# Three 512x512 products of a four-layer graph kernel as seven block products each, with streamed weights

## The chip, the cores and the metric

One core of a Trainium2 chip runs the whole kernel in one launch. The metric is the device time of that launch in microseconds. The kernel before took 2557.84 us (median of three runs, 2553.96 to 2559.38).

A core has five engines that run side by side, each through its own list of instructions in order: TensorE (PE; matrix products, with PEld for loading its stationary operand), VectorE (DVE), ScalarE (ACT), GpSimd (POOL) and SyncE (SP, which here only issues transfers). They wait for each other on semaphores. Matrix products land in PSUM, eight banks of 128 x 512 float32, which VectorE and ScalarE read.

## The reference

Four graph layers over 128 graphs of 64 nodes with 512 features, float32 throughout; after each layer the input is added and the sum normalised over the features:

```
x = layernorm(x + L0(x));  x = layernorm(x + L1(x));  ...  L3

L0: s = (x @ w) @ a
    A = exp(leaky(8 tanh((s_i + s_j)/8))) * adj          leaky(t) = t if t >= 0 else 0.1 t
    A = A / rowsum(A) * rowsum(adj);   out = A @ x @ w
L1: weight = adj * exp((x Wq^T + bq)(x Wk^T + bk)^T), rows divided by their sums
    out = weight @ (x Wv^T + bv)
L2: w_i = <q_i, (adj @ k)_i> / sqrt(512);   out = softmax(w) * (x @ Wv)
L3: two hypergraph convolutions with H = (adj != 0):
    conv(x, W, b) = Dn * (H @ (Be * (H^T @ (x @ W^T)))) + b
    h = layernorm(relu(conv(x, W1, b1)));   out = conv(h, W2, b2) + x
```

W1 is 1024 x 512 and W2 is 512 x 1024; the other weights are 512 x 512 (Wqk holds two).

## The kernel before

**Tiles and groups.** The 8192 node rows make 64 tiles of 128 rows (two graphs each); a group is two tiles (`GT = 2`), so there are 32 groups. A chunk is eight tiles, four groups; `prepare_chunk` works out what depends on `adj` alone for a chunk: `bhd` (H divided by both degrees), `am`, `radj` (the row sums of adj), `g1`.

**One group** is the generator `run(g)`, cut by `yield` into stages. Layer 0: scores and `exp`, placed on a block diagonal (`on_diagonal`, L474); the aggregation of x with it, transposed (`gathered`, L362), and the row sums by four matmuls with a column of ones (`row_sums`, L403), whose reciprocal times `radj` is the factor `f`; then the product with w0 (`product`, L370: per tile four accumulating matmuls of 128x128 by 128x512) and one VectorE instruction per tile that scales by `f` and adds x (L506); then `layer_norm` (statistics L459, L460, L450; the power on POOL, L452; L463). Layer 1: transposed x (`transposed`, L352), the row dot with `u1_b` on VectorE (L469), the bias added on POOL (L519); `product_T` with the prepared matrix m1 (L379, 16 matmuls of 256 columns); v by `product` with wv1, copied by ScalarE (L524); scores (L394), `exp`, and the aggregation (L537, L538). Layer 2: transposed x, `product_T` with m2, scores, a softmax over each graph (L565 to L579) that gives the factor `wc`, and v by `product` with wv2, scaled and added in one VectorE instruction per tile (L582). Layer 3: an aggregation, a product 512 to 1024 ("3a"), relu and normalisation, an aggregation (L626), a product 1024 to 512 ("3b"), the last `layer_norm`, the store.

**Seven products.** 3a and 3b already run in a form that uses seven block products in place of eight. Left and right side are cut into 2 x 2 blocks (left: two tiles by two halves of the contraction; right: two halves of the rows by two of the columns). `side_sums` (L408 to L411) forms four sums of left blocks, three on VectorE and one on POOL. The right sides, three plain blocks and four sums `t1` to `t4`, are made once at the start. `seven_products` multiplies pair by pair into PSUM: bank x (`chx`) collects three products in turn, z (`chz`) two, and the two y products go to the general banks `mm`. VectorE reads x after its first, second and third product, and z after each of its two; TensorE may add to a bank only after the read before.

**Streamed weights.** The seven right sides of 3a and 3b are 512 KB each. `fetch` loads them one after the other from DRAM, in the order of use, into a ring of six tiles on SP's queue; each product releases its tile and calls for the next fetch. w0, wv1 and wv2 stay in the core's memory for the whole run and are loaded at the start by POOL's queue. SP's queue also carries the loads of x and adj and the stores of the result.

**Order.** Four groups are in flight, four steps apart; in each step every group in flight goes on by one stage, in an order of ages that the loop writes out (youngest first, but in every fourth step the two oldest first). A scheduler in the language layer then sets the order on each engine, so matmuls of one stage stand between those of another; an engine goes through the resulting list strictly in order. PSUM: three banks `mm`, one `chx`, one `chz`, two `tr` (transposes and aggregations), one `sm` (small results).

Of the kernel before, what the change touches and what calls it, by code (L numbers as in the profile page):

```python
# [10 lines left out]
FP = mybir.dt.float32  # L11
# [4 lines left out]
P = 128  # L16
# [9 lines left out]
RING = 6  # L26
PIECE = 1024
EPS = 1e-5
# [5 lines left out]
def kernel(  # L34
# [99 lines left out]

    load_adj(0)
    load(0)
    w0_sb = weights(w0, D, D, "w0_sb")
# [10 lines left out]
    wv1_sb = weights(wv1, D, D, "wv1_sb")  # L148
    bv1_b = bcast(bv1, D, "bv1_b")
    wqk_g = wqk2.rearrange("(h c p) o -> h p c o", h=2, p=P)  # L150
    wv2_sb = weights(wv2, D, D, "wv2_sb")
# [22 lines left out]
    def prepare_0():  # L174

        u = small.tile([P, KC], FP, name="u0")
        for c in range(KC):
            row_dot(u[:, c : c + 1], w0_sb[:, c, :], 1.0, a0_b)
        ps = ps_mm.tile([P, D], FP, name="mm")
        for c in range(KC):  # L180
            nc.tensor.matmul(ps[:, ts(c, P)], u[:, c : c + 1].to_broadcast([P, P]), ident, start=True, stop=True)
        nc.scalar.copy(u0_b, ps)
# [35 lines left out]
    USE = ("b11", "b21", "t1", "t2", "b22", "t4", "t3")  # L218
    pieces = {}

    def piece_tile():
        return ring.tile([P, PIECE], FP, name="piece")

    def quarters(w, rows, cols):

        v = w.rearrange("(h c p) (i o) -> h i p c o", h=2, p=P, i=2)
        return {f"b{h + 1}{i + 1}": v[h, i] for h in range(2) for i in range(2)}

    def load_quarters(w, rows, cols):
        made = {}  # L230
        for name, src in quarters(w, rows, cols).items():
            made[name] = piece_tile()
            nc.sync.dma_start(out=made[name].rearrange("p (c o) -> p c o", o=cols // 2), in_=src)
        return made

    def combined(q):
        t1, t2 = piece_tile(), piece_tile()
        nc.gpsimd.tensor_sub(t1, q["b12"], q["b11"])
        nc.vector.tensor_sub(t2, q["b22"], t1)
        t3 = piece_tile()  # L240
        nc.gpsimd.tensor_sub(t3, q["b22"], q["b12"])
        t4 = piece_tile()
        nc.vector.tensor_sub(t4, q["b21"], t2)
        return {"t1": t1, "t2": t2, "t3": t3, "t4": t4}

    def stored(name, tiles):
        made = {}
        for k, t_ in tiles.items():
            made[k] = dram.tile([P, PIECE], FP, name=f"{name}_{k}")
            nc.sync.dma_start(out=made[k], in_=t_)  # L250
        return made

    def prepare_3a():
        q = load_quarters(w3a, D, DH)
        pieces["a"] = {**quarters(w3a, D, DH), **stored("w3a", combined(q))}

    def prepare_3b():
        q = load_quarters(w3b, DH, D)
        half = KH // 2

        ps = ps_mm.tile([P, D], FP, name="mm")
        for i in range(2):
            for c in range(KH):
                b = q[f"b{c // half + 1}{i + 1}"]
                nc.tensor.matmul(ps[:, ts(i, D // 2)], beta_c[:, c : c + 1].to_broadcast([P, P]),
                                 b[:, ts(c % half, D // 2)], start=(c == 0), stop=(c == KH - 1))
        nc.scalar.copy(bw_b, ps)
        for i in range(2):
            for c in range(KH):
                b = q[f"b{c // half + 1}{i + 1}"][:, ts(c % half, D // 2)]  # L270
                nc.vector.tensor_scalar(b, b, gamma_c[:, c : c + 1], None, ALU.mult)
        kept = stored("w3b", {k: q[k] for k in ("b11", "b21", "b22")})
        pieces["b"] = {**kept, **stored("w3b", combined(q))}
# [3 lines left out]
    fetched = [0]  # L277

    def fetch():
        n = fetched[0]  # L280
        fetched[0] += 1
        if n >= NG * 2 * len(USE):
            return
        which = "ab"[n // len(USE) % 2]
        src = pieces[which][USE[n % len(USE)]]
        t_ = piece_tile()
        dst = t_
        if len(src.shape) == 3:
            dst = t_.rearrange("p (c o) -> p c o", c=src.shape[1])
        nc.sync.dma_start(out=dst, in_=src)  # L290
        on_chip.append(t_)
# [14 lines left out]
    def prepare_chunk(c):  # L306
# [25 lines left out]
        bhd = chunks.tile([P, CT, N], FP, name="bhd")  # L332
        nc.gpsimd.tensor_mul(bhd, hA, per_tile(be))
        nc.gpsimd.tensor_mul(bhd, bhd, dn)
# [5 lines left out]

        am = chunks.tile([P, CT, N], FP, name="am")
        nc.gpsimd.tensor_mul(am, adj, per_tile(m))
        nc.vector.tensor_mul(am, am, over_graph(md))
        prepared[c] = adj, bhd, am, radj, g1
# [53 lines left out]
    def row_sums(e):  # L398

        ps = ps_sm.tile([P, GT, P], FP, name="sm")  # L400
        for t in range(GT):
            for h, (rows, _) in enumerate(halves):
                nc.tensor.matmul(ps[rows, t, 0:1], e(t, h), ones[rows], start=True, stop=True)  # L403
# [9 lines left out]
    def seven_products(a, s, base, dst):  # L413

        n = a["11"].shape[1]

        def times(ps, left, first, last):
            b = on_chip.popleft().rearrange("p (c o) -> p c o", c=n)
            for k in range(n):
                nc.tensor.matmul(ps, left[:, k, :], b[:, k, :], start=first and k == 0, stop=k == n - 1,  # L420
                                 skip_group_check=True)
            fetch()


        w = PIECE // n
        x = ps_ch.tile([P, D], FP, name="chx")[:, :w]
        y = ps_mm.tile([P, D], FP, name="mm")[:, :w]
        z = ps_ch.tile([P, D], FP, name="chz")[:, :w]
        add = nc.vector.tensor_add
        times(x, a["11"], True, False)  # L430
        add(dst["11"], x, base["11"])  # L431
        times(y, a["12"], True, True)
        add(dst["11"], y, dst["11"])
        times(z, s[0], True, False)
        add(dst["22"], z, base["22"])  # L435
        times(x, s[1], False, False)
        add(dst["12"], x, base["12"])
        times(z, s[3], False, True)
        add(dst["12"], z, dst["12"])  # L439
        y = ps_mm.tile([P, D], FP, name="mm")[:, :w]  # L440
        times(y, a["22"], True, True)
        add(dst["21"], y, base["21"])
        times(x, s[2], False, True)
        add(dst["22"], x, dst["22"])
        add(dst["21"], x, dst["21"])
# [25 lines left out]
    def on_diagonal(dst, e, adj):  # L471

        for rows, cols in halves:
            nc.vector.tensor_mul(dst[rows, :, cols], e[rows], adj[rows])  # L474
# [3 lines left out]
    def run(g):  # L478
        xt = xs.pop(g)
        adj, bhd, am, radj, g1 = prepared[g // GC]  # L480
        own = ts(g % GC, GT)
        adj, bhd, am, radj, g1 = adj[:, own], bhd[:, own], am[:, own], radj[:, own], g1[:, own]
# [15 lines left out]
        bd = on_diagonal(next_e(), e, adj)  # L498
        yield
        gT = gathered(xt, bd)  # L500
        f = small.tile([P, GT], FP, name="f")
        nc.vector.reciprocal(f, row_sums(lambda t, h: bd[halves[h][0], t, halves[h][1]]))
        nc.vector.tensor_mul(f, f, radj)
        yield
        for t in range(GT):
            nc.vector.scalar_tensor_tensor(xt[:, t, :], product(gT, t, w0_sb), f[:, t : t + 1], xt[:, t, :],  # L506
                                           ALU.mult, ALU.add)
# [202 lines left out]
```

## Time and profile before

| | |
|---|---|
| median of three runs | 2557.84 us |
| profiled execution | 2556.45 us |
| its span, first to last instruction | 2554.7 us |
| granted TensorE clock, mean | 0.995 |
| TensorE / weight loads busy | 2487.9 / 1644.5 us |
| VectorE / ScalarE / GpSimd busy | 1361.2 / 586.2 / 620.9 us |
| products with w0 (L370, 512 records) | 226.6 us |
| products with wv1 and wv2 (L370, 1024 records) | 450.6 us |
| HBM read / written | 266.65 / 22.54 MB |
| a 512 KB fetch, issue to landing | 4.1 to 4.3 us |

A line of the groups gives line, engine, operation, output<-input, shapes and count; then the busy time of the group in us and the mean length of one in ns; then the engine's idle time just before them and who ended it. Each float32 matmul of the program stands as two records of TensorE, so 768 matmuls of 512 columns are 1536 records. Matmuls are pipelined and a single length overlaps the next, so the price of a series is read from starts: the start of the next series less the start of this one.

A line of the timeline gives start and length in us, engine, line, operation, operands, how many instructions were merged, and in brackets the idle time ahead with its releaser.

### The profile page before, as it was taken

What the parts mean: (1) busy time and instruction counts of PE and PEld (TensorE: products, weight loads), DVE (VectorE), ACT (ScalarE), POOL (GpSimd) and SP (SyncE); (2) the same over time, 40 slices, a digit from 0 to 9 for tenths busy, and PEclk for the clock granted to TensorE, in tenths of its full rate; (3) what the DMA queues carried; (4) which work ended last, traced back from release to release, by engine and by line L of the source; (5) the groups of instructions that cost most, each with busy time, mean ns of one, the idle gap of its engine ahead of it and who ended that gap; (6) DMA issues with size and microseconds to landing.
All of it is one profiled execution on the core that took longest, in us unless ns stands there. A gap on an engine that the chain in (4) does not pass through costs nothing.

```text
span 2554.7 us, 31593 instructions
## 1 busy us (share of the span) xinstructions
PE 2487.9 (97%) x12440; PEld 1644.5 (64%) x12440; DVE 1361.2 (53%) x3012; ACT 586.2 (23%) x1164; POOL 620.9 (24%) x623
## 2 busy tenths in 40 slices
PE   6999999999999999999999999999999999999997
PEld 4466667666667666667666666666667666666665
DVE  3355455565545575445655545565544566544564
ACT  0122222222222222222222222222222222222221
POOL 4122222122222132222322223122212222212321
PEclk9999999999999999999999999999999999999999
DMA  7122332343232342233333242343233343233254
GB/s 256 33 108 85 110 128 85 126 132 100 95 132 86 120 145 83 99 132 102 117 124 100 91 136 91 115 132 110 84 129 100 107 132 116 86 120 117 77 179 140
DMA packets 102740, 291.24 MB, mean 114 GB/s; under 512 B 8944, under 2 KB 10992, under 8 KB 102592
## 3 DMA queue, kind: packets, MB, share of 16 engines
q1 hardware_dynamic: 100144, 280.53, 32.9%
q0 software_dynamic: 2448, 8.70, 1.0%
q8 instruction: 98, 1.61, 0.3%
q14 instruction: 50, 0.41, 0.0%
HBM read 266.65 MB, written 22.54 MB: 113 GB/s over the span
## 4 chain that ended last, share of the span: by engine, by line
PE 76%; DVE 10%; POOL 4%; issue 2%; DMA 2%; ACT 0%; POOLq 0%; DVEq 0%; ACTq 0%
PE mm L370 21%; PE mm L379 17%; PE chx L420 10%; PE chz L420 7%; PE mm L420 7%; PE tr L362 4%; PE tr L626 3%; PE sm L394 3%; DVE x L463 2%; POOL rstd L452 2%; DMA piece<-w3b_t 2%; PE tr L352 2%; PE mm L537 1%; POOL junk L593 1%; DVE ve L450 1%
## 5 line engine op out<-in xcount | busy, mean ns | idle before, releaser
L379 PE MATMUL mm<-xT,m_sb 128*128 128x256 f32 x2048 | 457.2, 381 | 3.8 <-DVE dn L325 3.4
L370 PE MATMUL mm<-wv_sb,xT 128*128 128x512 f32 x1024 | 450.6, 592 | 0.0
L379 PEld LDWEIGHTS mm<-xT,m_sb 128*128 128x128 f32 x2048 | 387.6, 190 | 73.8 <-issue 20.1
L370 PEld LDWEIGHTS mm<-wv_sb,xT 128*128 128x128 f32 x1024 | 191.8, 190 | 214.0 <-issue 212.1
L452 POOL TENSOR_TENSOR rstd<-ve,mhalf 128x2 f32<-128x2 f32 x160 | 124.5, 778 | 782.8 <-DVE ve L450 766.8
L420 PE MATMUL chz<-piece,h 128*128 128x256 f32 (+1 forms) x768 | 246.0, 455 | 15.0 <-DVE x L435 14.1
L542 DVE TENSOR_SCALAR hT<-adj 128x128 f32<-128x128 f32 x32 | 7.2, 228 | 468.0 <-PE sm L553 468.0
L370 PE MATMUL mm<-w_sb,xT 128*128 128x512 f32 x512 | 226.6, 594 | 0.0
L420 PEld LDWEIGHTS chz<-piece,h 128*128 128x128 f32 x768 | 143.0, 190 | 97.5 <-issue 51.7
L353 ACT COPY xT<-tr 128x512 f32<-128x512 f32 x128 | 68.9, 589 | 575.4 <-PE tr L352 575.4
L420 PE MATMUL chx<-piece,h 128*128 128x256 f32 (+1 forms) x640 | 181.3, 422 | 3.0 <-DVE x L431 2.1
L463 DVE TENSOR_SCALAR x<-x,mv,rstd 128x512 f32<-128x512 f32 x256 | 141.7, 595 | 76.1 <-POOL rstd L452 76.1
L459 DVE BATCH_NORM_STATS2 st<-x 128x6 f32<-128x512 f32 x256 | 176.1, 688 | 3.4
L370 PEld LDWEIGHTS mm<-w_sb,xT 128*128 128x128 f32 x512 | 97.3, 191 | 121.1 <-issue 120.9
L594 POOL TENSOR_SCALAR x<-x 128x512 f32<-128x512 f32 x64 | 44.1, 689 | 531.3 <-PE tr L362 531.3
L610 ACT ACTIVATE h<-h 128x512 f32<-128x512 f32 x128 | 80.6, 630 | 334.2 <-DVE h L439 151.9
L420 PEld LDWEIGHTS chx<-piece,h 128*128 128x128 f32 x640 | 121.4, 190 | 47.5 <-issue 30.1
L519 POOL TENSOR_TENSOR x<-x,bv_b 128x512 f32<-128x512 f32 x64 | 81.4, 1293 | 226.8 <-PE tr L352 223.9
L626 PE MATMUL tr<-g_bd,h 128*128 128x128 f32 x1024 | 123.3, 279 | 5.8 <-ACT h L617 5.8
L420 PE MATMUL mm<-piece,xT 128*128 128x512 f32 x256 | 128.7, 606 | 0.0
L626 PEld LDWEIGHTS tr<-g_bd,h 128*128 128x128 f32 x1024 | 120.4, 194 | 8.5 <-ACT h L617 8.1
L420 PE MATMUL mm<-piece,ghT 128*128 128x256 f32 x512 | 121.0, 379 | 0.0
(174 smaller groups left out, 3271.0 us busy)
## 6 DMA issues: line engine op xcount, KB each, us to landing
piece<-w3a_t SPq DMA_DIRECT2D x128, 512.0 KB, 4.3
piece<-w3b_t SPq DMA_DIRECT2D x128, 512.0 KB, 4.3
piece<-in_w3a_dram SPq DMA_DIRECT2D x100, 512.0 KB, 4.3
piece<-w3b_b SPq DMA_DIRECT2D x96, 512.0 KB, 4.1
x<-in_x_dram SPq DMA_DIRECT2D x32, 512.0 KB, 3.4
out_dram<-x SPq DMA_DIRECT2D x32, 512.0 KB, 2.8
adj<-in_adjT_dram SPq DMA_DIRECT2D x8, 256.0 KB, 3.6
wv_sb<-in_wv_dram POOLq DMA_DIRECT2D x2, 1024.0 KB, 18.7
```

The costliest lines, as they stand in the source:

```text
L353: nc.scalar.copy(xT[:, :, ts(t, P)], tr)
L362: nc.tensor.matmul(tr[:, c, :], xt[:, t, ts(c, P)], bd[:, t, :], start=True, stop=True)
L370: nc.tensor.matmul(ps, lhsT[:, k, ts(t, P)], w[:, k, cols], start=(k == 0), stop=(k == chunks - 1))
L379: nc.tensor.matmul(pz[:, : GT * P], w[:, k, ts(c, P)], xT[:, k, :], start=(k == 0), stop=(k == KC - 1))
L394: nc.tensor.matmul(ps[rows, t, :N], zT[:, k, tok], xT[:, k, tok], start=(k == 0), stop=(k == KC - 1))
L420: nc.tensor.matmul(ps, left[:, k, :], b[:, k, :], start=first and k == 0, stop=k == n - 1, skip_group_check=True)
L452: nc.gpsimd.tensor_tensor(rstd, ve, mhalf, ALU.pow)
L459: nc.vector.bn_stats(st[:, t, :], xt[:, t, :])
L463: nc.vector.tensor_scalar(xt[:, t, :], xt[:, t, :], mv[:, t, 0:1], rstd[:, t : t + 1], ALU.subtract, ALU.mult)
L519: nc.gpsimd.tensor_add(xt[:, t, :], xt[:, t, :], bv1_b)
L610: nc.scalar.activation(hi, hi, AF.Relu)
L626: nc.tensor.matmul(tr[:, c, :], h[:, t, ts(i * KC + c, P)], gm[:, t, :], start=True, stop=True)
```

## The change

Three further products take the seven-product form: w0 of layer 0, v of layer 1 and v of layer 2.

- `seven_products` gets functions for what is done with a finished block: `first` when a bank is read for a block's first part, `more` when something is added to it. For w0, v2 and layer 3 both are a VectorE instruction that scales the bank by a per-row factor and adds (`scaled_add`); for v of layer 1 `first` is a ScalarE copy and `more` a VectorE add. Bank z is filled second instead of third.
- `left_side` forms the side sums of these products in a tile `sums`, a stage ahead of the product.
- The right sides of w0 and both v are seven blocks of 256 KB, kept in DRAM two to a tile (four fetches a product); each group fetches them again. The ring has eight tiles. The fetch order over all groups is worked out ahead (`turns`, `to_come`).
- w0 and wv1 are loaded in halves into ring tiles and combined there (`prepare_first`); v2, 3a and 3b are loaded into the large tiles `h` by SP's queue, stored, combined in place and stored again (`prepare_later`). The combination has one subtraction on POOL and three on VectorE, where it had two and two.
- Layer 0: exp(A) * adj is summed over each graph by one matmul with the block matrix `same`, its reciprocal is taken over 128 x 128 and multiplied in before the aggregation, so the factor after the product is `radj` alone. That takes one stage more; the youngest group runs two stages in its first step.
- `bhd` becomes `bh` (one degree only); the other degree `dc` is a column and is multiplied in by `scaled_add` after the products of layer 3.

```diff
-RING = 6
+RING = 8
@@ seven_products
-        times(x, a["11"], True, False)
-        add(dst["11"], x, base["11"])
-        times(y, a["12"], True, True)
-        add(dst["11"], y, dst["11"])
-        times(z, s[0], True, False)
-        add(dst["22"], z, base["22"])
-        times(x, s[1], False, False)
-        add(dst["12"], x, base["12"])
-        ...
+        first("11", times(x, a["11"]))
+        first("22", times(z, s[0]))
+        more("11", times(ps_mm.tile([P, D], FP, name="mm"), a["12"]))
+        first("12", times(x, s[1], False))
+        more("12", times(z, s[3], False))
+        first("21", times(ps_mm.tile([P, D], FP, name="mm"), a["22"]))
+        u = times(x, s[2], False)
+        more("22", u)
+        more("21", u)
+    def left_side(xT):
+        a = left_blocks(xT)
+        room = work.tile([P, 4, KC // 2, P], FP, name="sums")
+        s = [room[:, i] for i in range(4)]
+        side_sums(s, a)
+        return a, s
+    def scaled_add(dst, ps, f, k, base):
+        t = int(k[0]) - 1
+        nc.vector.scalar_tensor_tensor(dst, ps, f[:, t : t + 1], base, ALU.mult, ALU.add)
@@ run, layer 0
-        bd = on_diagonal(next_e(), e, adj)
+        nc.vector.tensor_mul(e, e, adj)
+        yield
+        nc.tensor.matmul(ps, same, e.rearrange("p t i -> p (t i)"), start=True, stop=True)
+        rs = work.tile([P, GT, N], FP, name="e")
+        nc.vector.reciprocal(rs.rearrange("p t i -> p (t i)"), ps)
+        bd = on_diagonal(next_e(), e, rs)
         yield
         gT = gathered(xt, bd)
-        f = small.tile([P, GT], FP, name="f")
-        nc.vector.reciprocal(f, row_sums(lambda t, h: bd[halves[h][0], t, halves[h][1]]))
-        nc.vector.tensor_mul(f, f, radj)
-        yield
-        for t in range(GT):
-            nc.vector.scalar_tensor_tensor(xt[:, t, :], product(gT, t, w0_sb), f[:, t : t + 1], xt[:, t, :],
-                                           ALU.mult, ALU.add)
+        left = left_side(gT)
+        yield
+        seven_products(*left, *scaled_into(xt, radj))
@@ run, layer 1
+        left = left_side(xT)
         yield
         zT = product_T(xT, m1_sb, r1_c)
         v = work.tile([P, GT, D], FP, name="z")
-        for t in range(GT):
-            nc.scalar.copy(v[:, t, :], product(xT, t, wv1_sb))
+        at = blocks(v)
+        seven_products(*left, lambda k, ps: nc.scalar.copy(at[k], ps),
+                       lambda k, ps: nc.vector.tensor_add(at[k], ps, at[k]))
@@ run, layer 2
-            nc.vector.scalar_tensor_tensor(xt[:, t, :], product(xT, t, wv2_sb), wc[:, t : t + 1], xt[:, t, :],
-                                           ALU.mult, ALU.add)
+        left = left_side(xT)
+        yield
+        seven_products(*left, *scaled_into(xt, wc))
@@ combination of right sides
+    def combine(b, t):
+        nc.gpsimd.tensor_sub(t["t1"], b["b12"], b["b11"])
+        nc.vector.tensor_sub(t["t3"], b["b22"], b["b12"])
+        nc.vector.tensor_sub(t["t2"], b["b22"], t["t1"])
+        nc.vector.tensor_sub(t["t4"], b["b21"], t["t2"])
@@ order of the groups' stages, step by step
+        order = (0, 1, 2, 3, 0), (0, 1, 2, 3), (0, 1, 2, 3), (2, 3, 0, 1)
```

## The prediction

> **What bounds the kernel now.** I read the page first (engine shares, the slices, the chain that ended last), then TensorE's timeline for the price of each block of work, its idle gaps, and VectorE's timeline around those gaps. From the page:
>
> ```profile
> PE 2487.9 (97%) x12440; PEld 1644.5 (64%) x12440; DVE 1361.2 (53%) x3012; ACT 586.2 (23%) x1164; POOL 620.9 (24%) x623
> ...
> PE   6999999999999999999999999999999999999997
> ...
> PE 76%; DVE 10%; POOL 4%; issue 2%; DMA 2%; ACT 0%; POOLq 0%; DVEq 0%; ACTq 0%
> ...
> q1 hardware_dynamic: 100144, 280.53, 32.9%
> ```
>
> TensorE is full in every slice but the first and the last, and three quarters of the chain is its own work. VectorE is half busy, the transfers use a third of the DMA engines. So a column that TensorE need not stream is time, as long as nobody makes it wait. What a column costs, from TensorE's timeline (start, length, work; the pitch is the difference of two starts):
>
> ```profile
> 1239.20 1.89 PE L420 MATMUL mm<-piece,ghT 128*128 128x256 f32 x8
> 1240.93 1.89 PE L420 MATMUL chz<-piece,h 128*128 128x256 f32 x8
> ...
> 1260.16 7.07 PE L379 MATMUL mm<-xT,m_sb 128*128 128x256 f32 x32
> 1267.06 7.03 PE L370 MATMUL mm<-wv_sb,xT 128*128 128x512 f32 x16
> 1273.93 1.24 PE L379 MATMUL mm<-xT,m_sb 128*128 128x256 f32 x5
> ```
>
> Each written matmul is two records. 16 records of 512 columns take 1273.93 - 1267.06 = 6.87 us, 429.4 ns each; 32 of 256 columns take 6.90 us, 215.6 ns each, and the block products of L420 run at the same 1.725 us for 8. Half the columns, half the time, though every 256-column matmul loads its own weights.
>
> TensorE's only steady gap is one of 0.48 us in each round of four steps, where a block product wants a PSUM bank that VectorE has not read yet. Rounds without chunk preparation are 1169.56 - 1094.08 = 75.48 us apart:
>
> ```profile
> 1094.08 1.99 PE L420 MATMUL chz<-piece,h 128*128 128x256 f32 x8 [0.48 <-DVE x L435]
> ...
> 1169.56 1.99 PE L420 MATMUL chz<-piece,h 128*128 128x256 f32 x8 [0.50 <-DVE x L435]
> ```
>
> **The change, part by part.** The profiled execution took 2556.45 us (span 2554.7), 1.4 us under the median 2557.84; the sum is against 2556.45 and 1.4 is added at the end.
>
> *Products.* Per group and product, 16 records of 512 columns (6.87 us) become 28 of 256 (6.04): 0.833 us less. Three products, 32 groups: **-80.0 us**. All of it lies on TensorE's path.
>
> The Trainium skill, page "TensorE: Matmul & The Clock Gate", section "Back-to-back issue gap", speaks against this: it says that spacing is set by the weight load and the matmul together and gives sustained 81 ns at 128 columns and 131 at 512, so columns get dearer in narrow tiles. Read between (an estimate, 98 ns at 256), 28 narrow matmuls would cost 1.31 times 16 wide ones, and the term would be about +200 us instead of -80. The two timeline rows above decide for -80.
>
> *Normalisation ahead.* The row sums of layer 0 (L403, four matmuls of 64x1 per group, 0.3 us) go, one 128-wide matmul with `same` comes (L565 is its like, 0.32 us): nothing on TensorE. VectorE loses a reciprocal and a product of 128x2 (0.16 + 0.79) and gains a product of 128x128 (0.32) and a reciprocal of 128x128. For that the nearest rows are 3344 ns at 512 elements and 160 at 2, so 0.95 by a straight line (bounds 0.16 and 3.34). The column `dc` instead of `bhd` swaps one POOL product for another and adds a reduction of 0.68 per chunk.
>
> *VectorE's new work.* Per group: 8 scaled adds of 256 columns for w0 and for v2 in place of 2 of 512 (0.75 each). An unscaled add of 256 from PSUM takes 0.415, and scaling costs 0.06 at 512 columns (0.75 against 0.69), so 0.47: +2.26 twice. For v1 four adds (1.7; its four copies lie on ScalarE, which has room). Three side sums for each product: L408, L410 and L411 are 0.72, 0.65, 0.74: 6.3. The scaled adds of layer 3: +0.9. With the reciprocal some +13.7 us a group, 438 us in all: VectorE goes from 1361 to about 1800 us, 70% of the span. It does not become the bound by volume. But it works in order, and now runs nearly without a break through half of each round, while banks x and z serve five sets of products rather than two. So the price is waits. I followed the order of both engines in the changed program through one round, with start-to-start times of packed VectorE rows (0.60 for 512 columns, 0.38 for a scaled add of 256 by L435's 0.33 plus scaling, 0.66 for a row dot). Three places came out:
>
> A. The layer-0 gather now waits for the new reciprocal. The chain is hand-over 0.17, reciprocal 0.95, a side sum of layer 3 that stands ahead 0.43, the two diagonal blocks 0.30 each with another side sum (0.41) between: 2.56. TensorE has a block product (1.72) and seven score matmuls (0.47) to cover it. Wait 0.4; 0 if the sums were moved behind, 0.9 with the sums at the 0.72 and 0.65 of their means. Taken: **0.5**.
>
> B. Layer 2's value product wants bank x back after VectorE has gone through two layer norms, the softmax of layer 2 and three side sums. In the trace of before that stretch is measured:
>
> ```profile
> 1075.12 0.73 DVE L538 SCALAR_TENSOR_TENSOR x<-mm,f,x 128x512 f32<-128x512 f32 x1
> ...
> 1079.91 1.23 DVE L450 TENSOR_SCALAR ve<-mv 128x2 f32<-128x2 f32 x1
> ...
> 1086.40 0.75 DVE L582 SCALAR_TENSOR_TENSOR x<-mm,wc,x 128x512 f32<-128x512 f32 x1
> ```
>
> From L538 to L582 11.28 us; the new order adds a statistic (0.61), a row dot (0.66) and the first add itself (0.38): 12.93. It starts 0.7 us ahead of the layer-3 gather (L626), so bank x is free 12.2 us after that gather began. TensorE has in between the gather 3.62, four of v2's products 3.45, one of 3b's 1.725 and three transposes 2.6: 11.4. Wait 0.85; 0 where the two rstd waits in the stretch (0.21 and 0.57) swallow the additions, 2.2 if one more 128x2 operation takes 1.23 instead of 0.16. Taken: **0.9**.
>
> C. 3b's fourth product waits for the add behind v2's statistics and another row dot: nine scaled adds 3.42, three sums 1.26 to 2.1, statistics and the rest 2.1 to 2.7, together 6.9 to 8.2, against TensorE's 7.1. Wait 0 to 1.1, taken: **0.6**. The 0.48 of before stood here and goes.
>
> Places with under 0.3 us of slack (bank x between 3a and w0 among them): **0.3** together, bounds 0 and 1. Sum per full round 2.3 (0 to 5.2) in place of 0.48: +1.82, over 29 full rounds **+53 us**.
>
> Why sums cost between 0.34 and 0.83: with POOL idle a side sum of 256 columns takes 0.41 (L410 in a chunk round), with POOL at its own difference 0.80:
>
> ```profile
> 1050.48 0.80 DVE L408 TENSOR_TENSOR h<-xT 128x256 f32<-128x256 f32 x1 [2.36 <-ACT xT L363]
> ...
> 1266.52 0.41 DVE L410 TENSOR_TENSOR h<-h,xT 128x256 f32<-128x256 f32 x1
> ```
>
> The Trainium skill, page "GPSIMD Engine Reference", section "8. Key points", says that the two engines share SBUF interfaces and contend where VectorE has two SBUF inputs, as these sums do. With that rule on every new sum the three places go to their upper ends; with the idle row to their lower ones. POOL's three added differences (0.84 each) make the upper ends likelier.
>
> *Fetches.* 26 instead of 14 a group on SP's queue, 291 MB to about 425: the DMA share rises from 33% to some 48%. A piece lands in 4.3 us; in the new order each is asked for at least 7 us before its use, eight slots deep, and the output store and next x load stand in the queue where the fetches behind them are not wanted for 20 us. Cost 0; if that cover went, up to 4.3 us at one place a round.
>
> *Start and end.* wv2 moves from POOL's queue to SP's, w0 and wv1 load in halves, and v2, 3a and 3b are combined in place: VectorE's subtraction now stands in order behind a store (2.7 to 3.5) and a POOL difference (2.8 at 1024 columns), several times. TensorE's own gaps there were 28 us up to 82 us and 4.7 after. Bounds -8 (its gaps shrink, as early products have more to mix with) and +12 (two such blocks exposed), taken **+4**. Chunk rounds (six): one hand-over more, **+2**. The last group, alone: **+1**.
>
> **Sum:** -80 + 53 + 4 + 2 + 1 = -20: 2536.5, on the scale of the median **2538 us**. Each 1 us more of wait per round is 29 us; no change lies at 3.0 us of wait per round.
>
> **Rivals.** (1) Slower: the stretch at B is stretched by POOL, whose bias adds (1.29) and sums run beside it, as the 1.23 of L450 and 0.80 of L408 show. From 1.6 us at B the gain is gone; at 2.8 the round waits 4.2 us and the time is 2593. For it: VectorE is full there. Against: a backlog of this kind cost before only 0.48. (2) The cover holds everywhere, wait 0.9 a round: 2556 - 80 + 12 + 7, about 2497. For it: the order puts other products between. Against: VectorE's sums at B. (3) The narrow products do not run at 215.6 ns: at 238 (L420's 256-column records, busy time over count) 60 us are lost: 2598. Against: the starts above. (4) Pieces come late at one place: 2 us a round, 2596. Against: a third of DMA used.
>
> **How the numbers follow.** A change under 0.2% (5 us) is what a measurement of this kernel can hardly tell from none. Forecast 0.40 (waits 1.7 to 2.8 a round, 2520 to 2552); rival 2 0.14; no change (2.8 to 3.2) 0.08; rival 1 0.32; 3 and 4 0.03 each. Faster 0.54, same 0.08, slower 0.38. With one in ten left out at either end the range is 2504 to 2592.
>
> **What the profile after would show.** The three products at 6.04 us each; VectorE near 1800 us; TensorE's gaps on banks chx and chz behind VectorE, 2.3 us a round, the largest at v2's second use of chx; rounds of some 74.8 us; no gap on a piece. It is wrong if B alone passes 1.6 us, if the products' pitch is above 216 ns, or if TensorE waits for a transfer.

## The result: 4.5% slower, and the profile after

The changed kernel took 2672.8 us (median of four runs) against 2558.6: ratio 1.0447, 95% interval 1.0429 to 1.0465. I had forecast 2538 within 2504 to 2592. The page of the changed kernel:

```profile
span 2670.9 us, 35782 instructions
...
PE 2508.6 (94%) x13384; PEld 1898.2 (71%) x13384; DVE 1743.9 (65%) x3823; ACT 600.7 (22%) x1228; POOL 716.4 (27%) x721
...
q1 hardware_dynamic: 150656, 461.17, 51.5%
```

VectorE's volume came out as worked out (1744 us for about 1800). The transfers took 51.5% for some 48%; their bytes were undercounted (471 MB moved, 425 forecast: 21 blocks of 256 KB more for each of 32 groups are 176 MB on top of 291), but TensorE waited for none of them. TensorE, however, is less full than before, and its mean granted clock fell from 0.995 to 0.970. The groups of TensorE with idle time ahead of them (busy us, mean ns | idle us before, releaser) say where:

```profile
L454 PE MATMUL chx<-piece,sums 128*128 128x256 f32 x768 | 234.2, 433 | 77.1 <-DVE x L492 77.1
...
L454 PE MATMUL mm<-piece,ghT 128*128 128x256 f32 x512 | 121.3, 379 | 0.0
...
L396 PE MATMUL tr<-e_bd,x 128*128 128x128 f32 x512 | 66.5, 284 | 17.6 <-DVE e_bd L526 17.6
```

Two things are to be seen. 77.1 us are waits on bank x behind VectorE: the place that the prediction calls B. And the same shape, 128x256, has a mean of 379 ns in 3b's products and 433 ns in the series that follows those waits. TensorE's timeline of one round shows both:

```profile
1205.70 3.78 PE L683 MATMUL tr<-g_bd,h 128*128 128x128 f32 x32
...
1215.78 0.66 PE L386 MATMUL tr<-ident,x 128*128 128x128 f32 x4 [0.24 <-ACT xT L387]
1219.07 2.07 PE L454 MATMUL chx<-piece,sums 128*128 128x256 f32 x4 [2.64 <-DVE x L492]
1220.94 1.51 PE L454 MATMUL chz<-piece,sums 128*128 128x256 f32 x4
1222.29 0.27 PE L386 MATMUL tr<-ident,x 128*128 128x128 f32 x1
```

TensorE waits 2.64 us for bank x, and then four records that take 0.86 us elsewhere take 1220.94 - 1219.07 = 1.87, the next four 1.35. Over the 28 rounds with this wait the two series take 3.22 us on average (2.41 to 3.58), against 1.83 where the gap ahead of them is short (below). So a gap of 2.64 us costs on average another 1.4 us behind it.

**Where the time came from.** From the first layer-3 gather of h (L626, now L683) to the 30th are 29 rounds: 2206.6 us before, 2308.1 after, so 101.5 of the 116.2 us by which the span grew. The first of these gathers starts 11.3 us later, and from the 30th to the end of the program it takes 3.4 us more. In one round (75.47 us before, 78.68 after, no chunk preparation) TensorE's idle time grew from 0.50 to 3.65 us, while its busy time did not fall (74.98 and 75.03): the three products gave back 2.13 us at full clock, the slow series took 1.4, and the layer-1 aggregation (L593) took 2.84 in place of 1.84.

### The profile page after: what moved, and what is told of

Same layout as the page of the kernel before. It is cut to its first block, busy times and chain, and to the rows that moved or that the text cites. A ratio compares the mean times of both kernels' runs of the same rounds, so it can differ in the third digit from the quotient of the medians.

```text
span 2670.9 us, 35782 instructions
## 1 busy us (share of the span) xinstructions
PE 2508.6 (94%) x13384; PEld 1898.2 (71%) x13384; DVE 1743.9 (65%) x3823; ACT 600.7 (22%) x1228; POOL 716.4 (27%) x721
## 3 DMA queue, kind: packets, MB, share of 16 engines
q1 hardware_dynamic: 150656, 461.17, 51.5%
## 5 line engine op out<-in xcount | busy, mean ns | idle before, releaser
L454 PE MATMUL mm<-piece,xT 128*128 128x256 f32 (+1 forms) x1024 | 322.8, 437 | 3.2 <-DVE dn L356 3.2
L454 PE MATMUL chx<-piece,sums 128*128 128x256 f32 x768 | 234.2, 433 | 77.1 <-DVE x L492 77.1
L454 PE MATMUL chz<-piece,h 128*128 128x256 f32 (+1 forms) x768 | 252.2, 457 | 0.0
L454 PEld LDWEIGHTS chx<-piece,sums 128*128 128x128 f32 x768 | 156.2, 215 | 133.3 <-DVE x L492 85.1
L454 PEld LDWEIGHTS mm<-piece,xT 128*128 128x128 f32 x1024 | 193.2, 191 | 73.5 <-issue 47.4
L454 PE MATMUL chz<-piece,sums 128*128 128x256 f32 x768 | 220.9, 414 | 1.7 <-DVE x L492 0.9
L515 DVE TENSOR_SCALAR x<-x,mv,rstd 128x512 f32<-128x512 f32 x256 | 183.3, 757 | 49.8 <-POOL rstd L504 49.4
L454 PEld LDWEIGHTS chz<-piece,sums 128*128 128x128 f32 x768 | 162.2, 212 | 42.3 <-issue 9.1
L454 PE MATMUL chx<-piece,xT 128*128 128x256 f32 (+1 forms) x512 | 165.0, 443 | 0.3 <-ACT xT L387 0.3
L442 POOL TENSOR_TENSOR sums<-xT 128x256 f32<-128x256 f32 x96 | 93.9, 990 | 225.6 <-ACT xT L397 203.4
L683 PE MATMUL tr<-g_bd,h 128*128 128x128 f32 x1024 | 124.7, 281 | 8.5 <-ACT h L674 8.5
```

What stands on the lines that cost most here:

```text
L442: nc.gpsimd.tensor_sub(s[2], a["11"], a["21"])
L454: nc.tensor.matmul(ps[:, : b.shape[2]], left[:, k, :], b[:, k, :], start=start and k == 0, stop=k == n - 1, skip_group_check=True)
L515: nc.vector.tensor_scalar(xt[:, t, :], xt[:, t, :], mv[:, t, 0:1], rstd[:, t : t + 1], ALU.subtract, ALU.mult)
L683: nc.tensor.matmul(tr[:, c, :], h[:, t, ts(i * KC + c, P)], gm[:, t, :], start=True, stop=True)
```

## The experiments

Each ratio is against the kernel before as measured in the same session. Rounds are those without chunk preparation. "Series" is the time of the two series after bank x (chx, then chz), which is 1.83 us undisturbed; a dash where they don't follow such a wait.

| kernel | median us | ratio to before (95%) | round us | wait on bank x at v2 | series | clock |
|---|---|---|---|---|---|---|
| changed kernel | 2672.8 | 1.0447 (1.0429, 1.0465) | 78.7 to 80.4 | 2.63 | 3.22 | 0.970 |
| e1_no_bias_add | 2557.6 | 1.0017 (1.0007, 1.0026) | 75.40 | 0.73 | 1.82 | 0.993 |
| e2_v2_first_by_scalar | 2559.1 | 1.0020 (1.0011, 1.0029) | 75.13 | 0 | - | 0.993 |
| e3_v2_plain | 2609.7 | 1.0217 (1.0200, 1.0233) | 77.17 | 0 | - | 0.993 |
| e4_normalised_behind | 2631.0 | 1.0300 (1.0277, 1.0323) | 76.4 to 78.1 | 2.63 | 2.67 | 0.976 |
| e5_bias_later | 2558.0 | 1.0004 (0.9994, 1.0013) | 75.40 | 0.74 | 1.83 | 0.992 |
| e6_later_and_behind | 2529.7 | 0.9894 (0.9879, 0.9909) | 74.55 | 0.74 | 1.83 | 0.992 |
| e7_pairs_together | 2511.4 | 0.9821 (0.9806, 0.9835) | 73.89 | 0 (1.32 ahead of it) | - | 0.994 |
| e8_v1_wide | 2593.8 | 1.0147 (1.0132, 1.0162) | 76.36 | 1.16 | 1.82 | 0.993 |
| e9_dots_moved | 2520.4 | 0.9855 (0.9838, 0.9871) | 74.39 | 1.07 | 1.83 | 0.993 |
| e10_gap_made | 2549.1 | 0.9968 (0.9957, 0.9980) | 74.90 | 1.58 | 1.88 | 0.991 |
| e11_longer_gap | 2684.3 | 1.0502 (1.0486, 1.0518) | 79 to 80.5 | 3.77 | 3.39 | 0.967 |
| e12_next_dots_only | 2529.8 | 0.9898 (0.9881, 0.9914) | 74.59 | 1.22 | 1.83 | 0.993 |

### What makes the wait: e1, e5

My theory after the result was that POOL stretches VectorE's work ahead of v2's first add. Around that place POOL adds layer 1's bias (L573). e1 leaves that work out (x goes on without the bias of layer 1):

```diff
-        for t in range(GT):
-            nc.gpsimd.tensor_add(xt[:, t, :], xt[:, t, :], bv1_b)
         left = left_side(xT)
```

> The two additions of the bias of layer 1 on POOL (L573) are left out, so that POOL is idle where VectorE works toward the first add of v2; nothing else is changed. The theory (the wait of 2.64 us at v2's second use of bank x is a VectorE stretch made longer by POOL beside it, and the clock then falls for the products after it): the 128x2 add goes from 1.03 back to about 0.2 us, the row dot from 1.76 to 0.68, the wait from 2.64 to about 0.8 us, and the clock loss after it mostly goes: 2672.8 - 29 x (1.9 + 1.2) = about 2583 us, 2620 if POOL's side sum slides into the place of the bias add. The rival (the stretch is VectorE's own length, POOL does not matter): the wait stays above 2.3 us and the time within 2660 to 2673.

VectorE's timeline in the changed kernel ahead of v2's first add (L492):

```profile
1215.84 1.03 DVE L570 TENSOR_SCALAR d<-d,c_c 128x2 f32<-128x2 f32 x1
1216.79 0.15 DVE L635 TENSOR_TENSOR wc<-wc,sw 128x2 f32<-128x2 f32 x1
1216.86 1.76 DVE L521 SCALAR_TENSOR_TENSOR junk<-x,u_b 128x512 f32<-128x512 f32 x1
...
1218.55 0.47 DVE L492 SCALAR_TENSOR_TENSOR x<-chx,wc,x 128x256 f32<-128x256 f32 x1
```

POOL's timeline at the same time:

```profile
1215.19 1.66 POOL L573 TENSOR_TENSOR x<-x,bv_b 128x512 f32<-128x512 f32 x1 [3.45 <-DVE e L632]
1216.81 1.25 POOL L573 TENSOR_TENSOR x<-x,bv_b 128x512 f32<-128x512 f32 x1
1218.03 1.17 POOL L442 TENSOR_TENSOR sums<-xT 128x256 f32<-128x256 f32 x1
```

And VectorE in e1, the same instructions:

```profile
1162.02 0.22 DVE L570 TENSOR_SCALAR d<-d,c_c 128x2 f32<-128x2 f32 x1
...
1162.22 0.68 DVE L521 SCALAR_TENSOR_TENSOR junk<-x,u_b 128x512 f32<-128x512 f32 x1
...
1162.83 0.48 DVE L492 SCALAR_TENSOR_TENSOR x<-chx,wc,x 128x256 f32<-128x256 f32 x1
```

Beside POOL an addition of two numbers per partition takes 1.03 us instead of 0.22, and a row dot 1.76 instead of 0.68. That is 1.89 us, and the wait fell by 1.90. In an ordinary round 3.3 us went: the wait, and 1.4 of series that run at full clock again. Over the run 115 us went, the whole of the loss. It was more than expected (2583): the 29 rounds became 3.6 us shorter on average, where 3.1 were forecast, and another 9.0 us went ahead of the first layer-3 gather.

e5 keeps the additions and only puts them where VectorE is idle:

```diff
-        for t in range(GT):
-            nc.gpsimd.tensor_add(xt[:, t, :], xt[:, t, :], bv1_b)
         left = left_side(xT)
 ...
+        read = []
         seven_products(*left, lambda k, ps: nc.scalar.copy(at[k], ps),
-                       lambda k, ps: nc.vector.tensor_add(at[k], ps, at[k]))
+                       lambda k, ps: read.append(nc.vector.tensor_add(at[k], ps, at[k])))
+        for t in range(GT):
+            b = nc.gpsimd.tensor_add(xt[:, t, :], xt[:, t, :], bv1_b)
+            tc.add_manual_dep(b.ins, read[0].ins.name, ...)      # waits for it
```

> The changed kernel, complete, with only the place of POOL's two bias additions changed: they wait for VectorE's first addition to v of layer 1, some 26 us later, where VectorE has been idle. The theory (what the additions cost is the VectorE stretch that they run beside): the wait on bank x falls from 2.64 to about 0.75 us as without the additions, and the time to 2552 to 2565 us. The rival (POOL's time itself counts, wherever it lies): 2575 us or more, with a new wait near the place the additions move to.

2558.0, with the same wait as e1. So it isn't the amount of POOL's work but its place: 115 us for moving two instructions per group by some 26 us. The kernel is now level with the one before, not ahead of it.

### Around the wait, from the other side: e2, e3

e2 lets ScalarE read bank x, so that TensorE no longer waits for VectorE's stretch; POOL's additions stay where they were.

```diff
-        seven_products(*left, *scaled_into(xt, wc))
+        v = work.tile([P, GT, D], FP, name="z")
+        at = blocks(v)
+        seven_products(*left, lambda k, ps: nc.scalar.copy(at[k], ps),
+                       lambda k, ps: nc.vector.tensor_add(at[k], ps, at[k]))
+        for t in range(GT):
+            nc.vector.scalar_tensor_tensor(xt[:, t, :], v[:, t, :], wc[:, t : t + 1], xt[:, t, :],
+                                           ALU.mult, ALU.add)
```

> The value product of layer 2 takes the form of layer 1: ScalarE copies the first part of each block, VectorE adds the rest, and two more VectorE instructions scale by wc and add x. Bank x no longer waits for VectorE's stretch. The theory: the wait of 2.64 us on bank x and the slow products after it go, and the granted clock comes back to about 0.99; 2672.8 - 29 x (2.64 + 1.4) = about 2556 us, to which VectorE's two new instructions (0.66 each) may give back up to 30 us elsewhere. The rival (the wait moves whole to the next reader, because VectorE is late by the same amount everywhere): another wait of 2 us or more in each round and 2640 to 2675.

2559.1, as the theory had it; what is left is 0.53 us where 3b wants bank x back from VectorE, and the 0.77 at layer 0's gather. e3 gives up the seven parts for v2 alone:

```diff
-        seven_products(*left, *scaled_into(xt, wc))
+        for t in range(GT):
+            nc.vector.scalar_tensor_tensor(xt[:, t, :], product(xT, t, wv2_sb), wc[:, t : t + 1], xt[:, t, :],
+                                           ALU.mult, ALU.add)
```

> The value product of layer 2 alone goes back to eight wide products with its weights kept on the core; w0, v1 and the normalisation stay as in the changed kernel. The theory (wait at v2 and the clock drop that it triggers): 2672.8 - 29 x (2.64 + 1.4) + 32 x 0.83 = about 2582 us with a clock of 0.99 or more. A rival for the clock (it is low because the narrow products or their weight loads draw more, not because of the gap): the clock stays at 0.975 to 0.98 as two of three products are still narrow, and the time comes to 2672.8 - 77 + 27 = 2622 us or above.

The clock came back to 0.993 although two of three products are still narrow, so narrow products are not what lowers it. The time is 27 us over the theory's 2582. A wait that the theory did not hold more than covers this: bank z of 3b now stands 1.7 us a round behind VectorE, 49.2 us in all.

```profile
L455 PE MATMUL chz<-piece,h 128*128 128x256 f32 x512 | 124.1, 385 | 49.2 <-DVE x L493 49.2
```

### What the clock does after a gap: e10, e11

In e2 and e3 POOL's additions stay, the gap on bank x goes, and the clock comes back. The other side is a gap without those additions. For it I took e9 (below), where POOL's additions are elsewhere, and put useless VectorE work ahead of v2's first add: five instructions in e10, eight in e11.

```diff
+        late = work.tile([P, D], FP, name="junk")
+        for _ in range(5):                                       # e11: 8
+            wait = nc.vector.tensor_scalar(late, b3b_b, wc[:, 0:1], None, ALU.mult)
+        with tc.issue_after(wait.ins):                           # VectorE's adds behind it
             seven_products(...)
```

> The one before with five VectorE instructions of no use (128x512, some 0.5 us each) put ahead of v2's first add in every group, so that TensorE stands idle there for some 2 us without any work of POOL having been added. The theory (a clock that falls after an idle stretch of TensorE is a cost of its own): the series after the gap takes 1.1 to 1.9 us instead of 0.86 as in the changed kernel, the mean granted clock falls below 0.985, and a round grows by the gap and about 1 us beyond it. The rival (the slow series came from POOL or the transfers beside it): the series after the gap takes 0.86 to 1.0 us and the round grows by the gap alone.

> The kernel with the made gap, with eight useless VectorE instructions in place of five, so that the idle stretch grows by some 1.5 us, from 1.57 to about 3.1, longer than the 2.64 of the changed kernel, and again with no POOL work added. The theory (the clock falls once TensorE has been idle for longer than some 1.6 to 2.6 us): now nearly every series after the gap takes 1.1 to 1.9 us, the clock falls to 0.97 to 0.98, and a round grows by 1.5 us of gap and 1.0 to 1.4 us of slow clock, 2549 + 29 x 2.7 = about 2627 us. The rival (POOL's additions had slowed TensorE): the series stays at 0.97 us and the time comes to 2549 + 29 x 1.5 = about 2593 us.

The gap of e10 was shorter than planned, 1.58 us, and its series stayed at full clock in 29 of 30 rounds. The first round shown is the usual one, the second the one exception:

```profile
1228.86 1.13 PE L459 MATMUL chx<-piece,sums 128*128 128x256 f32 x4 [1.58 <-DVE x L498]
1229.83 1.03 PE L459 MATMUL chz<-piece,sums 128*128 128x256 f32 x4
...
1383.26 1.90 PE L459 MATMUL chx<-piece,sums 128*128 128x256 f32 x4 [1.58 <-DVE x L498]
1384.96 1.91 PE L459 MATMUL chz<-piece,sums 128*128 128x256 f32 x4
```

So e10 by itself told nothing against the rival. e11 did: its gap is 3.77 us, no POOL work came with it, and the series are slow in all of the 29 rounds with such a gap (2.89 to 3.58 us):

```profile
1128.11 2.07 PE L459 MATMUL chx<-piece,sums 128*128 128x256 f32 x4 [3.76 <-DVE x L498]
1129.97 1.91 PE L459 MATMUL chz<-piece,sums 128*128 128x256 f32 x4
```

Three more instructions, 2.2 us more gap, and 135 us more time: 29 x 2.2 is 64. Of the rest the slower series are 29 x 1.5 = 44, and a wait of 0.48 us that 3b gained is 13; 14 us are left open. Idleness alone lowers the clock. Put in a row by gap, of kernels in this case: 0.74, 1.07, 1.16, 1.22 and 1.7 us (e3) never slow; 1.58 once in 30 (with 0.24 of another wait close ahead of it); 2.63 in 23 of 28 rounds (e4) and 28 of 28 (the changed kernel); 3.77 in 29 of 29.

The gap's length alone does not decide, as e4 shows. The traces also hold the instants at which the granted clock changes. In every trace here they lie whole multiples of 3.413 us apart (to 0.01 us), so time falls into stretches of that length, each at full or at half clock. Rows of such stretches (start and end, length, TensorE's busy time and records, granted clock, DMA share, GB/s), first of the changed kernel, then of e4:

```profile
1215.09:1218.50 3.41, 1.11 (x9) 1.00 0.45 154
1218.50:1221.91 3.41, 2.84 (x7) 0.50 0.00 0
...
1192.78:1196.19 3.41, 2.40 (x17) 1.00 0.45 150
1196.19:1199.61 3.42, 1.56 (x7) 1.00 0.03 11
1199.61:1203.02 3.41, 3.41 (x18) 1.00 0.78 234
```

In the changed kernel TensorE is idle for 3.41 - 1.11 = 2.30 us of one stretch, and the next, in which the slow series lie, has half the clock. In e4 the same gap of 2.62 us falls on both sides of such an instant, 1.0 and 1.85 us of idle, and the clock stays full. This holds throughout: between 200 and 2370 us of all fourteen traces, the 81 full-speed stretches that a half-speed one follows hold 1.82 us of idle or more, and the 8719 others at most 1.85. A half-speed stretch was followed by another in 19 cases, with 0.66 us of idle or more in it, and by a full-speed one in 81, with 0.58 or less.

### The other two costs: e4, e6, e7

e4 normalises layer 0 behind the aggregation again; the bias additions stay in the bad place.

```diff
-        nc.vector.tensor_mul(e, e, adj)
+        bd = on_diagonal(next_e(), e, adj)
         yield
-        nc.tensor.matmul(ps, same, e.rearrange("p t i -> p (t i)"), start=True, stop=True)
-        rs = work.tile([P, GT, N], FP, name="e")
-        nc.vector.reciprocal(rs.rearrange("p t i -> p (t i)"), ps)
-        bd = on_diagonal(next_e(), e, rs)
         yield
         gT = gathered(xt, bd)
+        ...                      # four row sums of bd by matmul, f = radj / sums
-        seven_products(*left, *scaled_into(xt, radj))
+        seven_products(*left, *scaled_into(xt, f))
```

> Layer 0 is normalised behind the aggregation again (row sums by four matmuls, a 128x2 reciprocal, the factor multiplied in by the scaled adds); the product stays in seven parts and the stages stay where they are. The theory (the gather's wait of 0.77 us in 22 rounds is the new reciprocal ahead of it): that wait goes, with the slow clock after it, 22 x (0.77 + 0.4) = 26 us less, about 2647 us. The rival (the gather waits for VectorE's queue whatever is computed there): the wait stays within 0.2 us and the time within 2665 to 2680.

The gather's wait went, and the gain was 42 us instead of 26. The bank wait is the same 2.63 us, but the series after it now took 2.67 us on average instead of 3.22: 0.55 x 29 = 16 us that I had not counted. The stretches of 3.413 us show how that can be: a round of 78.12 us is 0.39 short of 23 of them (78.51), so from round to round the gap lies elsewhere on them, and the series fall by as much (3.26, 2.87, 2.49 us in three successive rounds); in 5 of 28 rounds they stay at full clock, in the changed kernel in none. So part of this gain hangs on the length of the round, not on the wait that was removed.

e6 puts e4 and e5 together, with no other edit.

> The bias additions later, and layer 0 normalised behind the aggregation. The theory (two separate waits, which add): 42 us less than with the additions moved alone, as that step gave by itself, about 2516 us; at least 22 x 0.77 = 17 us less if the clock effect that it also removed is already gone. The rival (the waits share one cause, VectorE's backlog, and one fix has had it all): within 5 us of the kernel with the additions moved alone.

2529.7, 28.3 less than e5: between the 17 for the wait alone and the 42. The round is 0.85 us shorter: 0.77 of wait, 0.32 of scores that the gather had cut in two, less some small changes.

e7 is e6 and keeps the four matmuls of the layer-1 aggregation together:

```diff
             po = ps_mm.tile([P, D], FP, name="mm")
-            for rows, _ in halves:
-                nc.tensor.matmul(po[rows], e[rows, t, :], v[rows, t, :], start=True, stop=True)
+            with tc.issue_after(w0_last[0]):     # the last matmul of the product with w0
+                for rows, _ in halves:
+                    nc.tensor.matmul(po[rows], e[rows, t, :], v[rows, t, :], start=True, stop=True)
```

> As the one before, and the four matmuls of layer 1's aggregation (64 rows each) are issued behind the last product of w0, so that no product stands between the two halves of a tile. In the changed kernel these eight records took 2.84 us a round, split two and six by a product, against 1.84 together in the kernel before. The theory (two matmuls on the two halves of the rows run side by side only when they are neighbours): 1.0 us a round, 29 to 32 us less than the one before. The rival (they are slower because of what runs beside them): within 8 us of the one before.

TensorE in the changed kernel, where a block product stands after the first two of eight records:

```profile
1201.48 1.05 PE L593 MATMUL mm<-z,e 64*64 64x512 f32 x2
1202.46 1.13 PE L454 MATMUL chx<-piece,sums 128*128 128x256 f32 x4
1203.52 1.93 PE L593 MATMUL mm<-z,e 64*64 64x512 f32 x6
1205.38 0.49 PE L621 MATMUL sm<-e,same 128*128 128x128 f32 x2
```

TensorE in e7:

```profile
1197.43 1.93 PE L603 MATMUL mm<-z,e 64*64 64x512 f32 x8
1199.30 0.49 PE L631 MATMUL sm<-e,same 128*128 128x128 f32 x2
...
1210.78 0.34 PE L545 MATMUL sm<-ident,s 128*64 128x64 f32 x4 [1.32 <-DVE junk L524]
```

Six records take as long (1203.52 to 1205.38) as all eight do together (1197.43 to 1199.30): two matmuls on the two halves of the rows overlap when they are neighbours, and the pair that is cut costs about 1 us more. The gain was 18 us, not 29 to 32. The third line tells why: in the order that came out, the next group's score matmuls stand ahead of bank x and wait 1.32 us for a row dot, where e6 had 0.74 and 0.24 of waits: 0.34 us a round, 10 us in all, were given back.

### What a single product is worth: e8

e8 is e6 with v of layer 1 as eight wide products:

```diff
-        seven_products(*left, lambda k, ps: nc.scalar.copy(at[k], ps), ...)
+        read = [nc.scalar.copy(v[:, t, :], product(xT, t, wv1_sb)) for t in range(GT)]
```

> The bias additions later, layer 0 normalised behind, and v of layer 1 alone back to eight wide products with its weights on the core: it prices one product, at a place where no engine waits. By the step of the forecast (0.833 us a product) it is 32 x 0.833 = 27 us slower than the kernel with seven parts. The rival (narrow products with a weight load each gain nothing): within 5 us of it.

64 us slower than e6, more than twice the forecast. The block itself is as worked out: the products with w0 and both v take 19.39 us a round against 18.57, 0.82 more. The rest is not the product: the wait on bank x grew from 0.74 to 1.16, 3b's bank x got one of 0.3 to 0.5, and chunk rounds are 2.5 us longer. The order of everything around it moved with the edit. So a difference of two kernels doesn't price a product here; starts in the timeline do.

### Two attempts to take the last wait: e9, e12

In e9 the row dots leave the stretch ahead of v2's first add (those of layer 1 behind its v, those of the next group behind v2's third add, its score matmuls behind v2's last product); in e12 only the next group's.

```diff
-            row_dot(s[:, t : t + 1], xt[:, t, :], 1.0, u0_b)
+        with behind(v2_add):                     # issued after v2's third add
+            for t in range(GT):
+                row_dot(s[:, t : t + 1], xt[:, t, :], 1.0, u0_b)
```

> All of the kernel, with the bias additions later, layer 0 normalised behind, the pairs together, and the row dots moved out of the VectorE stretch ahead of v2's first add: the two of layer 1 go behind VectorE's first addition to v of layer 1, where it is idle, with the bias additions after them; the two of the next group's layer 0 go behind v2's third add, and the score matmuls that read them behind v2's last product. The theory (what is left of the wait on bank x, and the 1.32 us wait on the row dot in the kernel before it, is VectorE's work ahead of the first add, some 2 us of it row dots): both waits go below 0.4 us together, 0.9 to 1.3 us a round less, 2474 to 2488 us. The rival (TensorE only reaches the bank earlier, because the scheduler moves the transposes behind it, and waits there or for the transposed x instead): within 10 us of 2511.

> The kernel with the pairs together, and of the row dots only those of the next group's layer 0 moved behind v2's third add, their score matmuls behind v2's last product; the row dots of layer 1 stay. The theory (one row dot less ahead of the first add, and no score matmul that makes TensorE wait 1.32 us for it): the wait on bank x falls to some 0.6 us and the round from 73.89 to about 73.2 us, 2490 to 2497 us. The rival (the transposes that the scheduler moves behind the bank cost as much as the wait gives, as when both pairs of dots were moved): 2505 to 2520 us.

Both missed, 9 and 18 us slower than e7 (e12 by more than its rival had it). VectorE did give bank x back sooner: in e7 it was taken 11.70 us after the gather began, in e12 11.06, in e9 10.03. But the scheduler then put fewer transposes ahead of bank x (none of sixteen in e9), so TensorE also arrives sooner and still waits 1.07 and 1.22 us, and in e12 bank z of 3b makes it wait 0.57 more:

```profile
1219.82 1.13 PE L459 MATMUL chx<-piece,sums 128*128 128x256 f32 x4 [1.22 <-DVE x L498]
...
1228.94 1.99 PE L459 MATMUL chz<-piece,h 128*128 128x256 f32 x8 [0.57 <-DVE x L498]
```

e7 remains the best, 2511.4 us: 1.8% faster than the kernel before, with all of its computation.

## Why the prediction was wrong

**Products, -80: right in the unit, a little large.** v of layer 1 stands undisturbed in the changed kernel, and takes 1247.48 - 1241.44 = 6.04 us:

```profile
1241.44 1.03 PE L454 MATMUL chx<-piece,xT 128*128 128x256 f32 x4
...
1247.48 7.07 PE L413 MATMUL mm<-xT,m_sb 128*128 128x256 f32 x32
```

All three take 18.57 us a round at full clock (e1) against 20.70: 2.13 less, not 2.50, since series after a wait or between other shapes cost some 0.1 more. That is -68 us.

**Wait B, 0.9: the step that failed.** It was 2.64, above its upper bound of 2.2 (whose own working, 0.85 and 1.07 for one slow operation, gives 1.9) and above the 1.6 that was named as the sign of being wrong. I had VectorE free bank x 12.2 us after the gather began; it was 13.37 (1219.07 - 1205.70). I had 11.4 us of other TensorE work; it was 10.73, because only part of the transposes stood ahead. Of the 1.17 us on VectorE's side more than all is POOL's bias addition (1.89 by e1). In the old trace it ran 24 us after the gather, beside a norm whose 128x2 addition took 1.27 us, and TensorE did not wait there; I did not follow where POOL's queue would put it in the new order. The contention went into the new side sums, and into the upper bound for one small addition, but not into the row dot. The first rival named exactly this mechanism and place, and I gave it 0.32.

The Trainium skill, page "GPSIMD Engine Reference", section "8. Key points", which the prediction weighed on the side sums alone, covers the row dot too, as it reads two operands from SBUF. The trace agrees: 1.76 against 0.68 us. Two operands are not all that counts, though: L502, a 128x2 addition that reads one tensor from SBUF, took 1.17 us at 1209.42 beside POOL's side sum, and 0.15 at 1207.21 without it. The trace also agrees for what the rule leaves out: the scaled adds, which read one operand from PSUM, have the same 0.47 to 0.48 us beside POOL and without it.

**The clock: a term that was missing.** The sum priced a wait at its length. At 2.64 us it cost 1.4 more a round, 41 us, since it left 1.82 us or more of idle in one stretch of 3.413. The Trainium skill, page "TensorE: Matmul & The Clock Gate", section "Why this matters for your kernels", warns of idle gaps over about 3 us between bursts of matmuls. Here a gap of 2.63 us was already enough in 28 of 28 rounds (23 of 28 in e4), and one of 1.58 in one of 30 (e10).

**Pairs cut apart: a second missing term.** The aggregation of layer 1 cost 1.0 us a round more and one set of scores 0.33, some 39 us in all; I had followed the order for waits only, not for what stands between neighbours.

**The other places.** A: 0.5 taken, 0.77 measured, in 22 of the rounds. The reciprocal was as estimated (957 ns for 950), but the two diagonal blocks took 628 ns on average instead of 300. C: 0.6 taken, 0 measured but for one 0.18. Others: 0.3 taken, 0.24 measured. No gap on a piece: the fetches cost nothing, as said, and the third and fourth rivals did not happen.

**Start and end.** The first layer-3 gather came 11.3 us later instead of 4; in e6, with the same loads and combinations, it came at 230.3 us, 5 earlier than before. With e1's edit alone it came 9.0 us earlier than in the changed kernel. So the start's own price is no loss, and most of the 11.3 is the same waits in the first rounds. Chunk rounds grew as the others did (78.99 to 82.05), so the 2 us for them were nothing of their own. The end cost 3.4 instead of 1.

**The sum again,** with what was measured, per round: -2.13 for the products, +3.15 of idle, +1.4 of slow clock, +1.33 for cut pairs; +3.75, against 3.2 to 3.5 from start to start. The remaining 0.3 to 0.5 us lies in small changes between other series, which I did not take apart. I had +1.82 - 2.50. Over the run, of the 135 us between 2538 and 2672.8, B took 50 (29 x 1.74), the clock behind it 41, the cut pairs 39 and the products 12; the other terms together gave back some 9. Without a price for the clock and the pairs the measured waits and products lead to some 2591 us, which is about where the first rival stood (2593).

## What to carry to other kernels

Before moving work so that one engine runs without a break, list what POOL does beside that stretch, in the new order, and price every instruction of the stretch for it; then look whether POOL's work has an idle stretch of VectorE to go to. Price an idle gap of TensorE that leaves some 1.8 us of idle in 3.4 us at its length and half as much again (2.64 us cost 1.4 more here), and read the new order for matmuls that were neighbours as well as for waits. Where a scheduler orders the list, a local edit moves the cover away with the wait, so an effect is read from starts in the timeline, not from the difference of two kernels.

## What the runs showed of the hardware that I had not expected

- A VectorE instruction of 128x2 took 1.03 us instead of 0.22 while POOL added 128x512 tiles, five times its length, where the row dot took 2.6 times its own. That looks like a wait for POOL rather than a lower rate: POOL's first addition ends at 1215.19 + 1.66 = 1216.85, this instruction at 1216.87; and POOL's side sum ends at 1210.56, the addition of L502 beside it (1.17 us) at 1210.59.
- The granted clock was set for stretches of 3.413 us at a time. Of the 82 at full clock with 1.82 us of TensorE idle or more 81 were followed by one at half clock, of those with less none. So what a gap costs depends on where it falls: the same 2.63 us gave 2.41 to 3.58 us for two series that take 1.83 at full clock, and in 5 rounds of e4 cost nothing beyond its length.
- Two matmuls on the two halves of the rows overlap almost fully as neighbours (eight records of 512 columns in 1.87 us); a block product between the first two ends that for this pair (2.84 us).
